# Attention head of a two-layer hybrid block: maxima of the first units spread over the projections of blocks one and two, later blocks projected beside the main line

## The chip, the cores and the metric

The kernel runs on one core of one Trainium2 chip. The metric is the device time of one launch in microseconds (us), as the median of several runs. The core has five engines with a queue each: TensorE (PE, with its weight loads shown apart as PEld), VectorE (DVE), ScalarE (ACT), GpSimd (POOL) and SyncE (SP), which here only issues DMAs. Matrix products land in PSUM, of which the kernel uses banks of 128 x 512 floats.

## The reference, cut to what matters

One sequence of 4096 rows of 256 features goes through attention, mixture of experts, attention, mixture of experts, each on a normalised input and added to its input. All is float32.

```python
def attn(x, Wq, Wk, Wv, Wo, bo, denom_bias):      # 16 heads of 16
    q, k, v = (split_heads(x @ W.T) for W in (Wq, Wk, Wv))
    sim = einsum('bhid,bhjd->bhij', q, k) / sqrt(16)
    sim = where(causal_mask, -max, sim)
    exp_sim = exp(sim - max(sim, -1))
    attn = exp_sim / (sum(exp_sim, -1) + exp(denom_bias))
    return merge_heads(attn @ v) @ Wo.T + bo
def ffn(x, phi_w, phi_b, expert_w, expert_b): ...  # soft mixture of 64 experts, 32 slots
x = x + attn_a(layernorm(x));  x = x + ffn(layernorm(x))
x = x + attn_b(layernorm(x));  x = x + ffn(layernorm(x))   # attn_b: no denom_bias, no bo
```

## The kernel before, in words

The four layers run one after the other on the same residual `x`, which stays in SBUF. The change touches only the class `_Attention`, which runs twice: attention a from about 0 to 1800 us and attention b from about 2650 to 4420 us of the profiled span.

**Blocks and units.** The 4096 rows are cut into eight blocks of 512. The 16 heads are cut into four groups of four. A unit is one group of heads of one block of query rows; the 32 units run block after block, four groups in each. A unit of block b looks at b + 1 key blocks, so the units grow.

**Projecting a block.** A block's rows are normalised, turned (8 transposes on PE), and multiplied by Wk, Wq and Wv: four `part`s, each two 128x512 products into one bank, and two `values`. Each `part` is split by ACT (L172) and DVE (L173) into a rounded and a rest term and written to DRAM (L175, L181), from where `load_to` (L337) reads it back in the layout of the scores, one 512 KB key tile or query tile at a time through SP's queue. `dense` (L234) is the list of seven steps that does this in one go, with the rows normalised on ACT. `pieces` (L186) is the same work as 16 small steps, with the rows normalised on POOL. These steps are put into `net.side`, and `net.beside` takes one of them at a time between the steps of the main line.

**Two passes over the scores.** `steps_a` (L359) computes the scores of a unit once for the row maxima: two 64-deep products into two banks, then two DVE reductions (L380 on the diagonal, L386 elsewhere) a step. After the last step `finish_a` turns the negated maxima and sends them through DRAM to the tile `qm`. `steps_b` (L438) computes the scores again into the tile `sc` with `-max` added by a second product, takes the exponential on ACT (L462), and `weigh` (L418) multiplies it with the values into `o`. So no unit's `steps_b` can begin before its maxima are done.

**Order around the change.** TensorE's instructions keep the order in which the program issues them (`net.mm` and `net.tr` pin it). The instructions of the other engines are placed by the framework's scheduler when their operands are ready. `wanted(n)` says how many steps of `steps_a` must be done by main step n; at n = 0 it is 16, the eight steps each of the first two units, which are both of block 0. Before the main line, `run` measures the rows (`net.stats` and `net.roots`, whose square root is on ACT), projects blocks 0 and 1 outright in attention a (`ready` is 0 there), and then runs blocks 2 and 3 as the list `front`, with one maxima step after each item. In attention b, blocks 0 and 1 were projected during the experts layer before (`ready` is 2), and `front` holds their values and blocks 2 and 3. In the main line, block b + 4 goes into `net.side` when block b begins. The banks of `steps_a`, of the projections and of the output product come from one pool of three; `sc` has two buffers.

Of the kernel before, what the change touches and what calls it, by code (L numbers as in the profile page):

```python
# [24 lines left out]
NQB = S // QB  # L25
# [17 lines left out]
class _Net:  # L43
# [5 lines left out]
    def __init__(self, ctx, tc, x, ident, eps):  # L49
        self.tc, self.nc = tc, tc.nc  # L50
        self.x, self.ident, self.eps = x, ident, eps
        pool = lambda n, b, **k: ctx.enter_context(tc.tile_pool(name=n, bufs=b, **k))
        cp = pool("net", 1)
        self.mv = cp.tile([P, NT, 2], F32, name="mv")
        self.rstd = cp.tile([P, NT], F32, name="rstd")
        self.shift = cp.tile([P, NT], F32, name="shift")

        self.zone = cp.tile([P, self.ZONE], F32, name="zone")
        self.stp = pool("stats", 4)
        self.ep = pool("ep", 1)  # L60
        self.dram = pool("dram", 1, space=DRAM)
        self.xds = [self.dram.tile([P, NT, D], F32, name=f"xd{n}") for n in range(2)]
        self.urgent, self.side = deque(), deque()
        self.agenda, self.now = [], 0
# [41 lines left out]
class _Attention:  # L106
# [12 lines left out]
    def __init__(self, net, name, wqT, wkT, wvT, woT, bo=None, db=None):  # L119
        self.net, self.name = net, name  # L120
        self.w = (wkT, wqT, wvT, woT)
        self.bo, self.db = bo, db
        self.kd, self.qd, self.ad = {}, {}, {}
        z = net.zone
        cut = lambda lo, n: z[:, lo : lo + n]
        self.wk, self.wq, self.wv = (
            cut(512 * n, 512).rearrange("p (c o) -> p c o", c=2) for n in range(3)
        )
        self.xb = [cut(1536 + 1024 * n, 1024).rearrange("p (c t) -> p c t", c=2) for n in range(2)]
        self.hl = [cut(3584 + 1024 * n, 1024).rearrange("p (l t) -> p l t", l=2) for n in range(2)]  # L130
        self.ys = [cut(5632 + 256 * n, 256) for n in range(2)]
        self.wo = cut(6144, 512).rearrange("p (c o) -> p c o", c=2)
        self.nhl = 0
        self.bot = None

    def load_weights(self):
# [49 lines left out]
    def pieces(self, b, fast=False, values=True):  # L186
        net, nc = self.net, self.net.nc
        xb, ys = self.xb[b % 2], {}
        idle = lambda: None

        def scale(i):
            if i == 0:
                self.begin(b)
            ys[i] = self.norm(4 * b + i, fast)

        def turn(t2):
            ps = net.bank().rearrange("p (c i t) -> p c i t", c=2, i=2)
            for i in range(2):
                for c in range(2):
                    net.tr(ps[:, c, i, :], ys[2 * t2 + i][:, ts(c, P)])  # L200
            nc.scalar.copy(xb[:, :, ts(t2, 2 * P)], ps.rearrange("p c i t -> p c (i t)"))

        def part(w, cc, key):
            ps = net.bank()
            for c in range(2):
                net.mm(ps, w[:, c, ts(cc, P)], xb[:, c, :], start=c == 0, stop=c == 1)
            self.split(ps, cc, (self.kd if key else self.qd)[b], key)

        out = []
        for t2 in range(2):  # L210
            out += [lambda i=i: scale(i) for i in (2 * t2, 2 * t2 + 1)]
            out += [idle, lambda t2=t2: turn(t2), idle]
        for w, key in ((self.wk, True), (self.wq, False)):
            out += [lambda a=(w, cc, key): part(*a) for cc in range(2)]
        if values:
            out += self.dense_values(b)
        return out
# [46 lines left out]
    def run(self, ready, at_end):  # L264

        net, tc, nc = self.net, self.net.tc, self.net.nc
# [3 lines left out]
        with ExitStack() as ctx:  # L270
# [13 lines left out]
                out=maskw, in_=maskw, compare_op=ALU.is_ge, fill=NEG,  # L284
# [11 lines left out]
            for p in range(2):  # L296
                f = net.ep.tile([P, QB], F32, name="ot", bufs=3)[:, 0:P]
                nc.gpsimd.memset(f, 0.0)
                for h2 in range(2):
                    for l in range(2):  # L300
                        nc.gpsimd.affine_select(
                            out=f, in_=f, compare_op=ALU.not_equal, fill=1.0,
# [34 lines left out]
            def load_to(n):  # L337
                while loaded[0] < min(n, len(kseq)):
                    u, kb = kseq[loaded[0]]
                    g, b = units[u]  # L340
                    if u not in qs:
                        q = qp.tile([P, 2, QB], F32R, name="q")
                        nc.sync.dma_start(
                            q.bitcast(F32),
                            self.qd[b][ts(g, HG)].bitcast(F32)
                            .rearrange("(p h) e l r t -> (h e l r) p t", p=2),
                        )
                        qs[u] = q
                    k = kp.tile([P, 2, QB], F32R, name="k")
                    nc.sync.dma_start(  # L350
                        k.bitcast(F32),
                        self.kd[kb][ts(g, HG)].bitcast(F32)
                        .rearrange("(p h) e r l t -> (h e r l) p t", p=2),
                    )
                    ks[u, kb] = k
                    loaded[0] += 1
# [77 lines left out]
            def values_to(n):  # L434
                while len(queue) > n:
                    weigh(queue.popleft())
# [107 lines left out]
            done_a = [0]  # L544

            def maxima_to(n):
                while done_a[0] < min(n, total):
                    next(runs)
                    done_a[0] += 1

            def wanted(n):
                for u in range(len(units)):
                    if due[u] > n:
                        lo, hi = due[u - 1], due[u]
                        first = ends[u - 1]
                        return first + -(-(ends[u] - first) * (n - lo) // (hi - lo))
                return total

            front = []
            if ready:  # L560
                for b in range(ready):
                    front += self.dense_values(b)
            else:
                for b in range(NQB):
                    for t in range(4 * b, 4 * b + 4):
                        net.stats(t)
                    net.roots(4 * b, 4 * b + 4)
                    if b < 2:
                        for f in self.dense(b, psb, prp):
                            f()  # L570
                    if b == 0:
                        load_to(1)
                if db is not None:
                    nc.scalar.activation(edb, edb, AF.Exp)
            for b in range(2, 4):
                front += self.dense(b, psb, prp)
            for f in front:
                f()
                maxima_to(min(done_a[0] + 1, wanted(0)))
            maxima_to(wanted(0))  # L580
            n = 0
            for u, (g, b) in enumerate(units):
                if g == 0 and 4 <= b + 4 < NQB:
                    net.side.extend(self.pieces(b + 4))
                if g == 0 and b == NQB - 1:
                    at_end()

                for p, _ in enumerate(steps_b(u)):
                    n += 1
                    if p % 2 == 0:  # L590
                        continue
                    while (
                        g >= 2 and net.side and u + 2 < len(units)
                        and units[u + 2][1] > max(3, b)
                    ):
                        net.beside()
                    want = wanted(n + 1)
                    maxima_to((done_a[0] + want) // 2)
                    values_to(1)
                    net.beside(2)  # L600
                    maxima_to(want)
# [555 lines left out]
```

## Time and profile before

| | |
|---|---|
| median of 3 runs | 5242.63 us (5239.64 to 5249.16) |
| the profiled execution | 5241.35 us, of which 5239.3 us from the first to the last instruction |
| PE busy | 5025.7 us (96% of the span) |
| DVE busy | 4141.6 us (79%) |
| ACT busy | 2633.1 us (50%) |
| mean granted TensorE clock | 0.982 |
| attention a: first main-line scores, last block ended | 84.5 us, 1793.5 us |
| attention b: first main-line scores, last block ended | 2717.4 us, 4412.3 us |

The profile has one row for an engine's group of instructions: the line of the kernel, the engine, the operation, the tile it writes and those it reads, how often, busy time, mean duration of one, and the idle time just before them with what ended it. A timeline row gives start, duration, engine, line, operation and tiles, and in brackets the idle time before it and its releaser. A row of a table by stage gives the stretch, its length, then the busy time (and number of instructions) of PE, PEld, DVE, ACT and, where all engines are asked for, POOL; then the granted TensorE clock as a share of full speed, the share of the DMA engines that were busy, and GB/s. A block's end is read from the copies of the finished output tile (L431), one a unit.

### The profile page before, as it was taken

What the parts mean: (1) busy time and instruction counts of PE and PEld (TensorE: products, weight loads), DVE (VectorE), ACT (ScalarE), POOL (GpSimd) and SP (SyncE); (2) the same over time, 40 slices, a digit from 0 to 9 for tenths busy, and PEclk for the clock granted to TensorE, in tenths of its full rate; (3) what the DMA queues carried; (4) which work ended last, traced back from release to release, by engine and by line L of the source; (5) the groups of instructions that cost most, each with busy time, mean ns of one, the idle gap of its engine ahead of it and who ended that gap; (6) DMA issues with size and microseconds to landing.
All of it is one profiled execution on the core that took longest, in us unless ns stands there. A gap on an engine that the chain in (4) does not pass through costs nothing.

```text
span 5239.3 us, 79442 instructions
## 1 busy us (share of the span) xinstructions
PE 5025.7 (96%) x29936; PEld 2683.4 (51%) x29936; DVE 4141.6 (79%) x7790; ACT 2633.1 (50%) x3108; POOL 1157.2 (22%) x1084
## 2 busy tenths in 40 slices
PE   7999999999999999989989999999999999999899
PEld 4444454445455344447754444545444553444488
DVE  5688989898989388767756889888889893787687
ACT  3466676766667622113224666766666676211132
POOL 3211100000000255534412111000000002555353
PEclk8999999999999999999999999999999999999999
DMA  6433222121121013433444332222121210134343
GB/s 252 140 107 127 67 73 68 61 67 61 59 64 53 32 78 104 148 127 114 144 175 144 107 127 67 72 68 64 64 64 57 64 53 31 77 105 147 122 148 111
DMA packets 266160, 499.16 MB, mean 95 GB/s; under 512 B 44944, under 2 KB 109968, under 8 KB 258096
## 3 DMA queue, kind: packets, MB, share of 16 engines
q1 hardware_dynamic: 260544, 485.57, 28.0%
q10 hardware_dynamic: 4896, 7.87, 0.4%
q8 instruction: 235, 3.85, 0.3%
q14 instruction: 149, 1.22, 0.1%
q0 software_dynamic: 336, 0.66, 0.1%
HBM read 336.73 MB, written 156.76 MB: 94 GB/s over the span
## 4 chain that ended last, share of the span: by engine, by line
PE 75%; DVE 11%; POOL 5%; issue 3%; ACT 3%; DMA 2%; SPq 0%; DVEq 0%; POOLq 0%; ACTq 0%
PE o L67 26%; PE bank L67 22%; PE sc L67 17%; PE acc L67 4%; DVE mx L386 4%; PE lg L67 4%; DVE junk L380 2%; POOL e L794 2%; PE ps L70 2%; POOL e L809 2%; ACT e L797 1%; DVE l L786 1%; ACT pb L462 1%; POOL e L826 1%; DMA zone<-ld 0%
## 5 line engine op out<-in xcount | busy, mean ns | idle before, releaser
L462 ACT ACTIVATE pb<-sc 128x1024 f32<-128x1024 f32 (+3 forms) x2304 | 2070.1, 950 | 1104.0 <-PE sc L67 1101.3
L386 DVE TENSOR_REDUCE mx<-bank 128x1 f32<-128x512 f32 x3584 | 2225.4, 682 | 179.5 <-PE bank L67 174.8
L67 PE MATMUL bank<-k,q 64*128 64x512 f32 (+3 forms) x4608 | 1354.7, 454 | 71.0 <-DVE mx L386 29.8
L67 PEld LDWEIGHTS bank<-k,q 64*128 64x128 f32 x4608 | 669.4, 186 | 1178.1 <-DVE mx L386 777.6
L67 PE MATMUL o<-pb,va 128*32 128x512 f32 (+3 forms) x9216 | 1160.4, 575 | 3.1 <-POOL pb L466 2.8
L67 PE MATMUL sc<-q,k 64*128 64x512 f32 (+3 forms) x4608 | 991.9, 391 | 9.6 <-ACT pb L462 9.2
L67 PE MATMUL sc<-qm,one 64*128 64x512 f32 (+3 forms) x4608 | 951.8, 378 | 0.0
L466 POOL TENSOR_SCALAR_AFFINE_SELECT pb<-pb 128x256 f32<-128x256 f32 x512 | 204.8, 407 | 2281.3 <-ACT pb L462 2275.5
L380 DVE CUSTOM_DVE_ANT_0 junk<-bank,maskw 128x128 bf16<-128x128 f32 (+3 forms) x1024 | 502.5, 491 | 258.9 <-PE bank L67 150.6
L67 PEld LDWEIGHTS sc<-q,k 64*128 64x128 f32 x4608 | 512.2, 187 | 138.2 <-ACT pb L462 98.9
L67 PEld LDWEIGHTS sc<-qm,one 64*128 64x128 f32 x4608 | 528.9, 187 | 67.7
L67 PE MATMUL acc<-e,x 128*128 128x512 f32 x1024 | 473.1, 605 | 19.3 <-POOL e L809 14.7
L797 ACT ACTIVATE e<-e 128x1024 f32<-128x1024 f32 x128 | 135.2, 1057 | 694.6 <-POOL e L794 694.6
L67 PE MATMUL lg<-zone,xnT 128*128 128x512 f32 x1024 | 463.3, 594 | 4.4 <-DVE l L786 3.8
L67 PE MATMUL o<-ys,lT 128*128 128x256 f32 x2048 | 464.9, 386 | 1.6 <-DVE xt L985 1.6
L67 PEld LDWEIGHTS o<-ys,lT 128*128 128x128 f32 x2048 | 392.6, 194 | 56.1 <-DVE xt L985 3.2
L826 POOL TENSOR_TENSOR e<-l,mc 128x1024 f32<-128x1024 f32 x120 | 281.3, 2365 | 319.5 <-DMA l<-ld 209.9
L67 PEld LDWEIGHTS o<-pb,va 128*32 128x32 f32 x9216 | 183.2, 108 | 290.6 <-issue 265.7
L67 PEld LDWEIGHTS acc<-e,x 128*128 128x128 f32 x1024 | 192.6, 193 | 265.5 <-issue 215.9
L809 POOL TENSOR_TENSOR e<-e,s 128x1024 f32<-128x1024 f32 x128 | 244.8, 1912 | 370.0 <-DVE s L808 348.5
L67 PEld LDWEIGHTS lg<-zone,xnT 128*128 128x128 f32 x1024 | 192.2, 190 | 245.7 <-issue 217.9
L807 DVE TENSOR_REDUCE s<-e 128x32 f32<-128x1024 f32 x128 | 156.1, 1219 | 155.2 <-ACT e L797 154.6
(122 smaller groups left out, 3208.4 us busy)
## 6 DMA issues: line engine op xcount, KB each, us to landing
k<-ak SPq DMA_DIRECT2D x144, 512.0 KB
k<-bk SPq DMA_DIRECT2D x144, 512.0 KB
ld<-l SPq DMA_DIRECT2D x128, 512.0 KB
l<-ld SPq DMA_DIRECT2D x60, 1024.0 KB
w<-in_L_ffn_expert_w_dram SPq DMA_DIRECT2D x26, 1024.0 KB
q<-aq SPq DMA_DIRECT2D x32, 512.0 KB
rb<-dd SPq DMA_DIRECT2D x64, 256.0 KB
q<-bq SPq DMA_DIRECT2D x32, 512.0 KB
```

The costliest lines, as they stand in the source:

```text
L67: self.tc.keep_in_program_order(self.nc.tensor.matmul(*a, **k))
L70: self.tc.keep_in_program_order(self.nc.tensor.transpose(o, i, self.ident))
L380: nc.vector.tensor_tensor_reduce(out=junk[:, 0:w], in0=scs[h2][:, 0:w], in1=maskw[:, QB - w : QB], scale=1.0, scalar=-3e38, op0=ALU.add, o ...
L386: nc.vector.tensor_reduce(m, scs[h2], AX.X, ALU.max)
L462: nc.scalar.activation(pb[:, :, off:QB], sc[:, :, off:QB], AF.Exp)
L466: nc.gpsimd.affine_select(out=d, in_=d, compare_op=ALU.is_ge, fill=0.0, base=0, pattern=[[0, 2], [1, P]], channel_multiplier=-1,)
L786: nc.vector.tensor_tensor(lf[:, ts(n, 512)], lg, phb[:, ds(h * EH + n * 512, 512)], ALU.add)
L794: nc.gpsimd.tensor_tensor(e, l, _bc(m.unsqueeze(2), [P, NH, SLOT]), ALU.subtract)
L797: nc.scalar.activation(ef, ef, AF.Exp)
L807: nc.vector.tensor_reduce(s, e, AX.X, ALU.add)
L809: nc.gpsimd.tensor_tensor(e, e, _bc(s.unsqueeze(2), [P, NH, SLOT]), ALU.mult)
L826: nc.gpsimd.tensor_tensor(e[:, ns, :], l, _bc(cms[t].unsqueeze(1), [P, NH, SLOT]), ALU.subtract)
```

## The change

The rows of blocks 3 to 7 of attention a are measured by a step of their own (`measure`) at the head of the block's `pieces`. Only block 0 is projected outright in attention a; blocks 1 and 2 form `front`, and the 16 maxima steps are spread evenly over its items. In attention b `front` is the values of blocks 0 and 1 and block 2. In the main line block b + 3 is projected beside block b, so block 3 moves from the head into block 0 of the main line, and each later block moves one block later. The amount of arithmetic stays the same.

```diff
@@ __init__
+        self.late = False
@@ pieces
-        out = []
+        def measure():
+            for t in range(4 * b, 4 * b + 4):
+                net.stats(t)
+            net.roots(4 * b, 4 * b + 4)
+
+        out = [measure] if self.late else []
@@ run
             else:
-                for b in range(NQB):
+                for b in range(3):
                     for t in range(4 * b, 4 * b + 4):
                         net.stats(t)
                     net.roots(4 * b, 4 * b + 4)
-                    if b < 2:
+                    if b == 0:
                         for f in self.dense(b, psb, prp):
                             f()
-                    if b == 0:
                         load_to(1)
+                self.late = True
                 if db is not None:
                     nc.scalar.activation(edb, edb, AF.Exp)
-            for b in range(2, 4):
+            for b in range(ready or 1, 3):
                 front += self.dense(b, psb, prp)
-            for f in front:
+            for n, f in enumerate(front):
                 f()
-                maxima_to(min(done_a[0] + 1, wanted(0)))
+                maxima_to(wanted(0) * (n + 1) // len(front))
             maxima_to(wanted(0))
             n = 0
             for u, (g, b) in enumerate(units):
-                if g == 0 and 4 <= b + 4 < NQB:
-                    net.side.extend(self.pieces(b + 4))
+                if g == 0 and b + 3 < NQB:
+                    net.side.extend(self.pieces(b + 3))
```

## The prediction

> **What bounds the kernel now.** I read the page first, then a table by stage (one row a block), then the timelines of PE and SP in the two heads.
>
> ```profile
> span 5239.3 us, 79442 instructions
> ...
> PE 5025.7 (96%) x29936; PEld 2683.4 (51%) x29936; DVE 4141.6 (79%) x7790; ACT 2633.1 (50%) x3108; POOL 1157.2 (22%) x1084
> ```
>
> PE is the bound: 214 us of the span are free of it, so a change that only moves PE work can win no more than the idle time it removes. Where is that idle time around the change?
>
> ```profile
> 28.50:42.70 14.20, 11.89 (x42) 6.90 (x40) 3.11 (x6) 7.10 (x13) 2.82 (x4) 1.00 1.03 385
> ...
> 85.00:100.00 15.00, 14.70 (x77) 8.00 (x73) 11.29 (x51) 5.20 (x8) 2.93 (x8) 0.56 0.21 76
> ...
> 84.50:165.40 80.90, 76.14 (x397) 38.84 (x397) 53.32 (x173) 28.71 (x45) 22.76 (x42) 0.73 0.39 132
> 443.90:642.00 198.10, 193.14 (x1356) 97.39 (x1353) 169.31 (x377) 125.17 (x148) 21.76 (x40) 1.00 0.33 105
> 642.00:870.60 228.60, 224.36 (x1636) 113.53 (x1633) 205.75 (x438) 151.34 (x173) 17.96 (x36) 1.00 0.22 69
> 1147.10:1465.10 318.00, 312.85 (x2276) 158.34 (x2273) 285.83 (x566) 213.45 (x237) 17.96 (x36) 0.99 0.20 63
> 2717.40:2791.60 74.20, 67.96 (x397) 35.64 (x396) 50.20 (x160) 30.74 (x48) 20.04 (x38) 0.84 0.43 135
> ```
>
> The first row is block 1 of attention a, projected outright: 14.2 us with 11.9 us of PE work. The next two show block 0 of a's main line at a granted clock of 0.56 and 0.73 while PE is hardly idle. The rows of blocks 3, 4 and 6 are the main line proper: PE idles about 5 us in each, with a projection beside it (block 3) or without (4 and 6). The last row is b's block 0: 6.7 us shorter than a's, at 0.84.
>
> ```profile
> 28.29 1.24 SPq L350 DMA_DIRECT2D k<-ak  x1
> 33.81 0.97 SPq L343 DMA_DIRECT2D q<-aq  x2
> ...
> 32.34 1.98 PE L67 MATMUL bank<-zone 128*128 128x512 f32 x4 [1.16 <-ACT zone L245]
> ...
> 44.96 0.33 PE L67 MATMUL bank<-k,q 64*128 64x128 f32 x2
> 46.18 1.98 PE L67 MATMUL bank<-zone 128*128 128x512 f32 x4 [0.89 <-ACT zone L245]
> ...
> 84.51 1.07 PE L67 MATMUL sc<-q,k 64*128 64x512 f32 x2
> ```
>
> This is a's head. The first query tile can only be asked for at 33.81, once block 0's queries are in DRAM. PE starts block 1's projections at 32.34, the first maxima at 44.96, the main line at 84.51.
>
> **Part 1, head of a.** The changed program's order on PE puts the first maxima right behind block 1's transposes, ahead of its first projection. PE keeps its order, so all of block 1's projections queue behind maxima that wait for the first key and query tile. When does the query land? Its issue takes half of 0.97 us, two 0.5 MB tiles are under way, and that stretch moves 385 GB/s, 1.3 us a tile: about 33.8 + 0.5 + 2.6 = 36.9, say 37. Bounds: 35.6 with one tile ahead, 40.3 if all five loads of that moment share the engines (6.5 us). The maxima of before began at 44.96 with no DMA named, so it cannot be later than that. From the first maxima on, before still did two blocks less one turn and 16 maxima steps; the changed head does the same. That took 84.51 - 44.96 = 39.55 us, of which 0.9 us was the wait for ACT's copy, done long before in the new order. So the main line starts near 37 + 38.65 = 75.7, a gain of 8.8 us (5.5 to 10.2) and not the 14.2 us of the block taken out: a wait of about 4.7 us (32.3 to 37) takes its place. Queued behind it on PE are block 1's projections, and with them ACT's and DVE's splits and SP's writes of that block; block 1's keys are first needed by the maxima of its own first unit, in the middle of block 0's main line, so only PE's own delay counts.
>
> **The clock after that wait.** What does such a gap do?
>
> ```profile
> 1810.49 6.05 PE L67 MATMUL acc<-e,x 128*128 128x512 f32 x8 [4.73 <-POOL e L809]
> ...
> 1808.40:1815.30 6.90, 4.81 (x6) 2.19 (x7) 5.37 (x7) 2.11 (x2) 4.98 (x4) 0.51 0.50 162
> ...
> 2361.24 1.02 PE L70 MATMUL ps<-ident,e 128*128 128x128 f32 x4 [2.03 <-DVE lT L884]
> ...
> 2361.40:2364.80 3.40, 3.40 (x11) 2.86 (x11) 3.40 (x6) 0.00 (x0) 0.56 (x1) 0.50 0.29 120
> ```
>
> A gap of 4.73 us is followed by some 5 us of work at half clock (0.51), one of 2.03 us by 3.4 us at 0.50. The Trainium skill, "TensorE: Matmul & The Clock Gate" (section "Why this matters for your kernels"), warns only of idle gaps over about 3 us, and holds some 4 us of continuous work enough for full clock. By the rule the new gap costs one slow stretch and no more. By the rows it costs 3.4 to 5 us at half rate, 1.7 to 2.5 us, and busy work is no protection: the row 85 to 100 is 98% busy and stays at 0.56. I take +1.7 us, and keep 0 and +7 (the difference of the two blocks 0 above) as ends for what shifted work does to the slow stretches.
>
> **Part 2, block 3 beside the main line.** Blocks 0 to 3 of the main line each had one projection beside them and still have one; block 4 gets one that it had not. PE works 96% and more of every block, so this costs about its PE time: 11.9 us by the row above. A second way: blocks 4 and 6, without side work, differ by 89.4 us or 44.7 a block, so block 3 without its side work would be 183.9; it took 198.1, hence 14.2. I take 12.5 us (11 to 14.5). Its DVE work (four splits of 0.69 us), ACT copies and POOL normalising (four of 1.23 and four of 0.73 us) lie in engines with 23 us and more of slack in that block. Its six DMA issues queue on SP, where block 3 carried the same six between its key loads. Sum for a: -8.8 + 1.7 + 12.5 = **+5.4 us**.
>
> **Part 3, `measure`.** Read from the source it would put a square root, and so two table loads (1.28 us each in the trace), between exponentials five times: 12.8 us of ACT. In the changed program's order all 32 row measurements on DVE and all eight roots on ACT still stand in the head, in the places of before, and ACT's count of table loads is unchanged. Cost zero, unless the chip's order were another; the cover is the scheduler.
>
> **Part 4, head of b.** Here keys and queries are loaded long before, so no wait appears.
>
> ```profile
> 2698.12 0.66 PE L70 MATMUL sc<-ident,zone 128*128 128x128 f32 x4
> ...
> 2717.37 0.50 PE L67 MATMUL sc<-q,k 64*128 64x512 f32 x2
> ...
> 2720.54 0.38 PE L67 MATMUL bank<-k,q 64*128 64x256 f32 x1 [0.25 <-DVE mx L380]
> 2721.11 0.38 PE L67 MATMUL bank<-k,q 64*128 64x256 f32 x1 [0.20 <-DVE mx L380]
> ```
>
> Block 3's stretch, 2698.12 to 2717.37, is 19.25 us and goes. Its maxima do not: 11 items now carry 16 steps, so five steps follow another maxima step directly, and there the three banks free up at DVE's pace, 0.57 us a bank at 256 wide (0.44 at 128 and 0.84 at 512 in the rows around it). A step is two banks; the five are 256, 512, 128, 384 and 512 wide: 1.15 + 1.6 + 0.9 + 1.35 + 1.6 = 6.6 us. Gain 19.25 - 6.6 = 12.6 us (11 to 14). Block 3 beside the main line costs 12.5 as in a. Sum for b: **-0.1 us**.
>
> **Total.** +5.3 us. Against the profiled execution (5239.3 span + 2.05 around it = 5241.35) that is 5246.7; the median of the runs shown is 1.3 us higher, so 5248.
>
> **Rivals.** (1) The slow clock spreads. After the wait PE runs at half rate into thin work, and b's first block, now behind paired maxima, starts cold as a's does (0.73 and not 0.84). Place: the first 80 us of each main line; price 6.7 us for b and up to 3 more for a's head, so about 5258, slower. For it: 98% busy work stayed at 0.56; b's slow stretch begins only at 0.51 around 2740. Against it: before's b also has waits of 0.7 us in every head step and keeps 1.00. It decides from one extra slow stretch of 13 us. (2) The slow clock shrinks: a's first block starts warm as b's does, gaining 6.7 us there and about as much in block 1 (122.3 us in a, 115.8 in b), and the new side work finds PE's idle time in block 4 (4.2 us). About 5235. For it: the lone maxima steps ahead of a's main line fall from two to one. Against it: the rest of that stretch is the same. (3) The change does nothing, because what leaves the head returns in full: then 5243 to 5245, the low half of my own case. (4) `measure` does land between the exponentials: +13 us or more; the order speaks against it.
>
> **How the numbers follow.** Chances: my sum 0.57, rival 1 0.25, rival 2 0.15, rival 4 0.03. My own case spans 5240 to 5256 from the bounds above. To leave out no more than 2 in 10 the range must take half of each rival: 5236 to 5262. A measurement of this kernel can tell about 0.2%, 10.5 us, from no change: below 5232 counts as faster, above 5253 as slower. From my case 0.17 lies above 5253 and 0.01 below 5232; rival 1 gives 0.21 above, rival 2 0.07 below, rival 4 lies above. Faster 0.08, same 0.51, slower 0.41.
>
> **What would show it.** In the profile after: PE's wait of 4 to 6 us before the first `bank<-k,q` row near 37 us; a's first `sc<-q,k` near 76 and b's about 26 us after its transposes of block 2 (39.4 before, from 2677.97); block 4 of both attentions longer by 11 to 14 us, near 241; blocks 3, 5 and 6 within 2 us; no new table load between exponentials. I am wrong if block 4 grows by under 8 us, if a's head gains over 12 us, or if the granted clock of the two blocks 0 moves by over 0.1.

## The result, and the profile after

The changed kernel takes 5253.05 us (median of 12 runs, 5246.8 to 5259.35) where the kernel before took 5238.93 us in the same measurement (12 runs, 5225.59 to 5249.16). The ratio is 1.0029, with a 95% interval of 1.002 to 1.0039: slower by 14 us (10.5 to 20.4), more than twice the forecast 5 us. The profiled execution took 5252.87 us; the kernel before had 5241.35.

The page of the changed kernel, engines' busy time (`...` marks lines left out, here and below):

```profile
span 5251.2 us, 79427 instructions
...
PE 5032.9 (96%) x29936; PEld 2684.6 (51%) x29936; DVE 4140.1 (79%) x7790; ACT 2629.6 (50%) x3102; POOL 1166.8 (22%) x1092
```

PE has the same 29936 instructions. Its busy time grew by 7.2 us and its idle time (span less busy) from 213.6 to 218.3 us. The change was to win idle time back; it added some. Where? The table by stage of the changed kernel (stretch, length, then busy time of PE, PEld, DVE, ACT and POOL, granted clock, DMA share, GB/s):

```profile
28.50:43.00 14.50, 6.08 (x19) 2.62 (x17) 0.93 (x6) 4.57 (x8) 2.81 (x4) 0.69 1.02 390
34.20:47.90 13.70, 8.65 (x14) 3.15 (x14) 1.71 (x9) 0.83 (x2) 0.00 (x0) 0.51 0.83 319
...
83.10:160.40 77.30, 70.77 (x388) 35.26 (x389) 52.79 (x172) 28.93 (x45) 23.25 (x43) 0.82 0.39 137
433.30:632.80 199.50, 194.60 (x1356) 98.18 (x1353) 169.45 (x377) 125.11 (x148) 25.59 (x44) 0.99 0.28 89
632.80:876.90 244.10, 238.60 (x1676) 120.99 (x1673) 208.55 (x442) 156.10 (x181) 21.76 (x40) 0.99 0.28 94
1150.60:1468.40 317.80, 312.72 (x2276) 158.52 (x2273) 285.68 (x566) 213.48 (x237) 17.94 (x36) 0.99 0.20 63
2710.90:2786.10 75.20, 68.86 (x397) 36.21 (x397) 52.62 (x170) 29.46 (x47) 20.04 (x38) 0.84 0.43 140
3258.80:3505.60 246.80, 239.09 (x1676) 120.83 (x1673) 208.05 (x438) 156.06 (x181) 20.35 (x38) 0.99 0.29 93
```

Rows one and two are a's head: PE does 6.08 us of work in 14.5 us, and then runs at a granted clock of 0.51 for 13.7 us. The rows that start at 433.30 and 1150.60 are blocks 3 and 6, as long as before (198.1 and 318.0). The rows at 632.80 and 3258.80 are block 4 of a and of b: 244.1 and 246.8 us where block 4 took 228.5 and 228.4. The rows at 83.10 and 2710.90 are the two blocks 0; b's kept its length and clock (74.2 us, 0.84).

The timeline of SP and that of PE in a's head, changed kernel:

```profile
33.68 0.99 SPq L350 DMA_DIRECT2D q<-aq  x2
34.72 0.46 SPq L357 DMA_DIRECT2D k<-ak  x1
```

```profile
38.85 0.47 PE L67 MATMUL bank<-k,q 64*128 64x128 f32 x2 [7.28 <-DMA q<-aq]
39.26 3.78 PE L67 MATMUL bank<-zone 128*128 128x512 f32 x4
...
43.84 3.78 PE L67 MATMUL bank<-zone 128*128 128x512 f32 x4 [0.39 <-DVE mx L387]
...
48.47 1.98 PE L67 MATMUL bank<-zone 128*128 128x512 f32 x4 [0.53 <-DVE mx L387]
...
57.33 1.99 PE L67 MATMUL bank<-zone 128*128 128x256 f32 x8 [0.65 <-DVE mx L387]
...
64.14 3.28 PE L67 MATMUL bank<-zone 128*128 128x512 f32 x4 [0.85 <-ACT zone L252]
...
83.10 0.73 PE L67 MATMUL sc<-q,k 64*128 64x512 f32 x2
```

The query tile asked for at 33.68 lets PE go on at 38.85, after a wait of 7.28 us. The same `part` (two products into a bank, `bank<-zone` 128x512 x4 here, as each product is two records) takes 3.78 us at half clock and 1.98 us at full clock: two parts right behind the wait are slow, and one more at 64.14 is slow in part (3.28 us). So the main line starts at 83.10, only 1.4 us earlier than before, although a block of 14.2 us has left the head.

The timeline of PE in b's head, changed kernel:

```profile
2685.92 0.66 PE L70 MATMUL sc<-ident,zone 128*128 128x128 f32 x4
...
2689.81 3.50 PE L67 MATMUL bank<-zone 128*128 128x512 f32 x4 [0.30 <-DVE mx L387]
...
2710.89 0.73 PE L67 MATMUL sc<-q,k 64*128 64x512 f32 x2
```

From the transposes of block 2 to the first scores it is 24.97 us, 39.4 before, although one part here too runs at half clock (3.50 us). What is block 4 paying? PE's groups in a's block 4 of the changed kernel (shapes, count, busy us and mean ns, idle time before and its releasers):

```profile
L67 PE MATMUL bank<-k,q 64*128 64x512 f32 x289 | 90.0, 473 | 5.1 <-DVE mx L393 3.5 <-DVE mx L387 0.3 <-DVE zone L175 0.2
...
L67 PE MATMUL bank<-zone 128*128 128x512 f32 x16 | 7.9, 618 | 0.0
...
L67 PE MATMUL bank<-zone 128*128 128x256 f32 x16 | 4.0, 392 | 0.0
...
L70 PE MATMUL bank<-ident,zone 128*128 128x128 f32 x8 | 1.3, 287 | 0.0
```

The last three rows are the new side work: 7.9 + 4.0 + 1.3 = 13.2 us of PE. PE's busy time in the block grew by 14.2 us (238.60 against 224.36); the maxima (the first row) ran 0.6 us longer and waited 1.4 us longer for their banks than in the kernel before:

```profile
L67 PE MATMUL bank<-k,q 64*128 64x512 f32 x289 | 89.4, 468 | 3.7 <-DVE mx L386 2.1 <-DVE mx L380 0.3
```

### The profile page after: what moved, and what is told of

Same layout as the page of the kernel before. It is cut to its first block, busy times and chain, and to the rows that moved or that the text cites. A ratio compares the mean times of both kernels' runs of the same rounds, so it can differ in the third digit from the quotient of the medians.

```text
span 5251.2 us, 79427 instructions
## 1 busy us (share of the span) xinstructions
PE 5032.9 (96%) x29936; PEld 2684.6 (51%) x29936; DVE 4140.1 (79%) x7790; ACT 2629.6 (50%) x3102; POOL 1166.8 (22%) x1092
## 4 chain that ended last, share of the span: by engine, by line
PE 75%; DVE 11%; POOL 4%; issue 3%; DMA 3%; ACT 3%; SPq 0%; DVEq 0%; POOLq 0%; ACTq 0%
PE o L67 26%; PE bank L67 22%; PE sc L67 17%; PE acc L67 5%; PE lg L67 4%; DVE mx L393 4%; DVE junk L387 2%; POOL e L802 2%; PE ps L70 2%; POOL e L817 1%; ACT e L805 1%; DVE l L794 1%; ACT pb L469 1%; DMA zone<-ld 1%; DMA l<-ld 1%
## 5 line engine op out<-in xcount | busy, mean ns | idle before, releaser
L67 PEld LDWEIGHTS lg<-zone,xnT 128*128 128x128 f32 x1024 | 192.3, 190 | 245.1 <-issue 219.0
```

The source lines that it names most:

```text
L67: self.tc.keep_in_program_order(self.nc.tensor.matmul(*a, **k))
```

## The experiments

Each kernel of the table was timed beside runs of the kernel before on the same chip; rows with the same median of before share those runs. One profile shows single stages to a few us only: two profiles of the unchanged kernel have a's block 0 at 80.9 and 76.4 us and a's end at 1793.5 and 1785.3. Block 4 (228.4 to 228.5 us in both attentions) and a's head (39.5 us from first maxima to first scores) repeat much better, and most verdicts rest on those. b's head took 47.7 us in one and 50.6 us in the other: in the second, two parts ran at half clock.

| kernel | median, us | before, us | ratio (95%) | first scores of a | a's block 4 | b's head | b's block 4 |
|---|---|---|---|---|---|---|---|
| before | 5238.93 | | | 84.5 | 228.5 | 47.7 | 228.4 |
| changed | 5253.05 | 5238.93 | 1.0029 (1.002 to 1.0039) | 83.1 | 244.0 | 34.1 | 246.8 |
| e1, b alone | 5240.04 | 5237.1 | 1.0004 (0.9996 to 1.0013) | 85.8 | 229.5 | 34.0 | 243.6 |
| e2, a alone | 5250.23 | 5237.1 | 1.0029 (1.0015 to 1.0043) | 84.3 | 246.3 | 47.7 | 228.6 |
| e3, no wait | 5248.16 | 5237.1 | 1.0022 (1.0015 to 1.003) | 73.1 | 243.9 | 33.9 | 245.4 |
| e5, warm gap | 5256.58 | 5237.1 | 1.0036 (1.0024 to 1.0049) | 83.9 | 245.1 | 34.2 | 246.4 |
| e4, side work twice | 5268.26 | 5235.03 | 1.0061 (1.0048 to 1.0073) | 85.3 | 243.5 | 47.7 | 244.6 |
| e6, spread alone | 5246.57 | 5235.03 | 1.0024 (1.0017 to 1.003) | 88.3 | 228.4 | 45.5 | 228.2 |
| e7, warm gap, old pacing | 5246.85 | 5235.03 | 1.0025 (1.0017 to 1.0033) | 77.8 | 248.4 | 32.5 | 247.8 |
| e8, all in the head | 5258.72 | 5235.03 | 1.0043 (1.003 to 1.0055) | 140.9 | 229.8 | 106.0 | 228.6 |
| e9, before again | 5237.79 | 5236.76 | 0.9999 (0.9991 to 1.0007) | 85.5 | 228.5 | 50.6 | 228.4 |
| e10, spread in a | 5240.94 | 5236.76 | 1.0005 (0.9997 to 1.0013) | 91.0 | 228.6 | 47.7 | 228.2 |
| e11, change, old pacing in a | 5250.41 | 5236.76 | 1.0029 (1.0019 to 1.004) | 79.9 | 243.6 | 34.2 | 245.1 |

The columns of block 4 and of b's head are in us; b's head runs from its first maxima to its first scores.

**One attention at a time.** e1 keeps attention a as before and changes b; e2 does the reverse. Of e1 (e2 swaps the conditions, and has the changed head in a):

```diff
-            for b in range(2, 4):
+            for b in range(2, 3 if ready else 4):
...
-                maxima_to(min(done_a[0] + 1, wanted(0)))
+                maxima_to(
+                    wanted(0) * (n + 1) // len(front) if ready
+                    else min(done_a[0] + 1, wanted(0))
+                )
...
-                if g == 0 and 4 <= b + 4 < NQB:
-                    net.side.extend(self.pieces(b + 4))
+                ahead = 3 if ready else 4
+                if g == 0 and b + ahead < NQB:
+                    net.side.extend(self.pieces(b + ahead))
```

> Attention b as in the changed kernel, attention a as before. Theory (each attention trades a cheaper head for 15 to 18 us of projections beside block 4): b alone is +7 us, near 1.0013, with its first scores about 34 us after its first maxima (47.7 before) and its block 4 at 245 us. Rival (the loss is a's late query and slow clock alone): b alone is within 2 us of before.

> Attention a as in the changed kernel, attention b as before. Theory: +6 us, near 1.0011; a's first scores near 83, its block 4 at 244 us, and this and the other half add up to the +14 us of the whole. Rival (the loss is b's): within 2 us of before.

Measured: b alone costs 2 us (-2 to 7), a alone 15 us (8 to 23), and together they make up the whole. Neither 7 nor 6 us came: b's half is what its rival said, and nearly all of the loss is a's. In e2's profile the main line starts at 84.34 and block 4 is 246.3 us: the block came back and the head gave nothing for it. In b the head gives 13.7 us and block 4 takes 15 to 18 us, a little more than that.

**The wait taken out.** e3 is the changed kernel with a's maxima begun only when block 1's projections have been issued, seven items later, so that the query has landed by then:

```diff
-                maxima_to(wanted(0) * (n + 1) // len(front))
+                skip = 0 if ready else 7
+                maxima_to(wanted(0) * max(0, n + 1 - skip) // (len(front) - skip))
```

> The changed kernel, but in attention a no maxima step is issued until block 1 is projected; all 16 are spread over block 2's seven items. So nothing of block 1 queues behind the first query tile. Theory (the wait of 7.3 us and the half clock after it ate the head's gain): a's first scores near 75 in place of 83.1, and the total 8 us under the changed kernel, near 5245. Rival (PE idle time only moves: nine more paired maxima steps wait for banks at 1.3 us each, and thin work turns the clock down anyway): first scores at 80 to 84, total within 3 us of the changed kernel.

Measured: 5248.16, by the ratios some 4 us under the changed kernel, where 8 were expected, and still 11 us (8 to 16) over before. The profiled execution took 5240.49 us, one of e3's quickest, so only its stages are read here. PE's timeline and its stage row in e3:

```profile
46.10 0.43 PE L67 MATMUL bank<-k,q 64*128 64x128 f32 x3
...
73.07 1.08 PE L67 MATMUL sc<-q,k 64*128 64x512 f32 x2
```

```profile
46.10:73.10 27.00, 20.65 (x66) 9.95 (x65) 16.49 (x66) 5.81 (x8) 4.42 (x5) 1.00 1.03 380
```

Without the wait the clock stays at 1.00 and the main line starts at 73.07, 12 us ahead of before. So the wait and the half clock in the head cost the changed kernel 10 us there. But block 4 still takes its 15 us more, and that is over what even this head gives.

**The gap kept warm.** e5 is the changed kernel with eight useless products (7 us of PE) in the place of the idle wait:

```diff
+                if n == 0 and not ready:
+                    warm = psb.tile([P, 2, QB], F32, name="sc")
+                    for _ in range(8):
+                        mm(
+                            warm[:, 0, :], self.wk[:, 0, 0:P], self.xb[0][:, 0, :],
+                            start=True, stop=True,
+                        )
```

> The changed kernel with eight products of no use (128x512, 6.9 us at full clock, result dropped) put on PE into a's wait for the first query tile. Theory (the wait turned the clock down): the first two projections after it take 1.98 us each and not 3.78, the granted clock from 30 to 48 us stays at 1.00, a's first scores come at 78 to 79 in place of 83.1; total 4 us under the changed kernel. Rival (the thin interleaved work itself turns the clock down): half clock there as before, first scores at 83 or later.

The timeline of PE and a stage row of e5:

```profile
32.27 7.03 PE L67 MATMUL sc<-zone 128*128 128x512 f32 x16
39.23 0.33 PE L67 MATMUL bank<-k,q 64*128 64x128 f32 x2
39.49 1.99 PE L67 MATMUL bank<-zone 128*128 128x512 f32 x4
...
53.79 1.99 PE L67 MATMUL bank<-zone 128*128 128x256 f32 x8 [0.66 <-DVE mx L387]
55.72 0.50 PE L67 MATMUL bank<-k,q 64*128 64x512 f32 x2
56.46 1.04 PE L67 MATMUL bank<-k,q 64*128 64x512 f32 x2 [0.24 <-ACT va L235]
...
60.60 3.78 PE L67 MATMUL bank<-zone 128*128 128x512 f32 x4 [0.85 <-ACT zone L252]
```

```profile
60.00:74.00 14.00, 12.49 (x18) 4.29 (x18) 3.27 (x17) 1.92 (x4) 3.84 (x5) 0.51 0.69 269
```

The first part behind the gap is now fast (1.99 us), so it was the idle wait that had slowed it. Yet the half clock comes 20 us later, at 60, where PE had no gap over 0.85 us, and the main line starts no earlier (83.86). Nor is the total the 4 us lower that were expected. Something else in the new head turns the clock down. What differs from the head of before at that place is the pacing: the even spread puts two maxima steps in a row (55.72 and 56.46) ahead of block 2's transposes, so between the end of the last projection (53.79 + 1.99 = 55.78) and the next (60.60) lie 4.8 us of maxima and transposes alone. In the kernel before it was 62.47 to 66.00, 3.5 us:

```profile
60.48 1.99 PE L67 MATMUL bank<-zone 128*128 128x256 f32 x8 [0.66 <-DVE mx L380]
...
66.00 1.98 PE L67 MATMUL bank<-zone 128*128 128x512 f32 x4 [0.68 <-ACT zone L245]
```

**The spread alone, and the old pacing.** Four kernels test that. e6 is the kernel before with the spread alone; e10 has it in a only; e7 is e5 with the old pacing in a; e11 is the changed kernel with the old pacing in a and nothing warmed. e6's edit, and that of e11 (e10 and e7 are made of the same lines):

```diff
-                maxima_to(min(done_a[0] + 1, wanted(0)))
+                maxima_to(wanted(0) * (n + 1) // len(front))
```

```diff
-                maxima_to(wanted(0) * (n + 1) // len(front))
+                maxima_to(
+                    wanted(0) * (n + 1) // len(front) if ready
+                    else min(done_a[0] + 1, wanted(0))
+                )
```

> The kernel before, with only the maxima spread evenly over the projections of blocks two and three (one step after each second or so item to the end, instead of one after each item until all are done); the same blocks are projected in the heads. Theory: the spread by itself brings nothing, -1 to 0 us, first scores of a 0 to 1 us earlier. Rival (the clock decides): thinner interleaving at the end turns PE's clock down in other places, and block 0 of a's main line moves by over 3 us either way.

> The kernel before with the even spread of the maxima in attention a alone; b keeps one step after each item. Theory (the spread costs through the half clock it brings to a's head, 68 to 75 us in the profile with the spread in both): first scores of a 42 to 43 us after the first maxima instead of 39.5, total 3 to 11 us over before, as much as with the spread in both. Rival (b's spread is what costs): total within 2 us of before.

> The changed kernel with the useless products in a's wait and, in a, the old pacing of the maxima (one step after each item, so no two steps stand directly before block 2's turn). Theory (the paired maxima with the turn turn the clock down near 60 us): no stretch at half clock at 60 to 74 us, first scores near 78 us, total 5 us under the changed kernel, about 5248. Rival (it is the thin work of maxima between projections as such): the half clock comes at another place of the head, first scores at 82 us or later, total 5253 to 5257.

> The changed kernel with the old pacing of the maxima in a (one step after each item until done), nothing warmed. Theory (the spread cost a some 8 us, and the prediction had put it at nothing): about 8 us under the changed kernel, 5243 to 5246 where before has 5236; the half clock after the wait stays (34 to 48 us), the one at 65 us goes, first scores near 79 to 80 us. Rival (the wait turns the clock down anyhow, and the pacing is of no account): first scores at 83 us, total within 3 us of the changed kernel, ratio to before 1.0025 or more.

The timeline of PE in e6, then in e11, then a stage row of e7:

```profile
60.96 2.00 PE L67 MATMUL bank<-zone 128*128 128x256 f32 x8 [0.66 <-DVE mx L380]
...
67.78 2.96 PE L67 MATMUL bank<-zone 128*128 128x512 f32 x4 [0.85 <-ACT zone L245]
...
71.53 3.78 PE L67 MATMUL bank<-zone 128*128 128x512 f32 x4 [0.39 <-DVE mx L380]
```

```profile
39.20 0.47 PE L67 MATMUL bank<-k,q 64*128 64x128 f32 x2 [7.88 <-DMA q<-aq]
39.60 3.78 PE L67 MATMUL bank<-zone 128*128 128x512 f32 x4
...
55.86 1.99 PE L67 MATMUL bank<-zone 128*128 128x256 f32 x8 [0.65 <-DVE mx L387]
...
61.38 1.98 PE L67 MATMUL bank<-zone 128*128 128x512 f32 x4 [0.68 <-ACT zone L252]
...
79.88 0.73 PE L67 MATMUL sc<-q,k 64*128 64x512 f32 x2
```

```profile
60.00:74.00 14.00, 11.53 (x38) 5.32 (x37) 7.66 (x30) 2.93 (x5) 2.55 (x3) 1.00 0.88 343
```

In e6, the kernel before with nothing but the new pacing, the pause is 62.96 to 67.78 (4.8 us) and two parts behind it are slow (2.96 and 3.78 us instead of 1.98). In e11 and e7, the pause is 3.5 us (57.85 to 61.38 in e11) and the clock stays up. At this place, the second turn to a new block in a's head, every profile agrees: with the spread begun at a's first item (changed, e2, e5, e6, e10) the half clock comes, at 60 to 71 us, five times out of five; with the old pacing (before, e1, e4, e7, e8, e9, e11) never.

The length of the pause alone does not decide, though. In e3 a pause of 4.1 us (57.27 to 61.38) left the clock at 1.00. And e10 fell to half clock already at 47, behind the pause of 3.25 us (43.01 to 46.25) one block earlier, where before, e1, e4, e6, e8 and e9, whose program is the same up to there, did not. The timeline of PE in e10:

```profile
46.25 2.93 PE L67 MATMUL bank<-zone 128*128 128x512 f32 x4 [0.89 <-ACT zone L245]
...
49.98 3.78 PE L67 MATMUL bank<-zone 128*128 128x512 f32 x4 [0.39 <-DVE mx L380]
```

Of the 45 pauses of 3.2 to 3.7 us in the heads of the thirteen profiles, four were followed by half clock (e10 here, e8 in both heads, e9 in b's). In b's head with the change the pause is 4.2 us, and half clock follows in five profiles of six; in the sixth, e7, the head is some 1.5 us shorter. Over these profiles, then, a longer pause makes half clock likelier, and chance has a part.

In a, the pacing moves the first scores by some 2 to 6 us: 77.80 against 83.86 (e7 and e5), 88.3 against 85.5 (e6 and e9). Of the 3.2 us between e11 and the changed kernel (79.88 and 83.10), 1.8 belong to half clock that lasted longer behind the wait, and of the 5.5 us of e10 (91.0) some 2.8 to the two slow parts above.

The Trainium skill, "TensorE: Matmul & The Clock Gate" (section "Part 1: The HAM clock gate (the "warmup" mystery)"), says that the gate watches PE's activity in free-running windows of some 3.4 us. The record of the granted clock agrees: half-clock stretches here last 3.4 us or a multiple of it (6.8, 10.2, 13.7 us). A pause of 4.8 us can fill such a window with light work, and one of 3.2 to 3.5 us only where it happens to lie right; that this is the reason is my reading, only the effect of the pacing at that place is shown.

The totals don't resolve 4 us. By their ratios e7 is 13 us over before where e5 was 19, but only 2 us under the changed kernel, where 5 were expected. e11 missed: 5243 to 5246 was expected, 5250.4 measured, no different from the changed kernel within the intervals (10 to 21 us over before, against 10.5 to 20.4), although its trace does what the theory said. e6's theory, -1 to 0 us, fell, and its total is a riddle: 12.6 us over before (9 to 16), of which its stages show 3 to 4 in a's head and none in b (its b head is even 2.2 us shorter), while e10, with the same spread in a, measures 3 us (-2 to 7), which cannot choose between its theory (3 to 11) and its rival (within 2). That remainder is open.

**The price of a side block.** e4 is the kernel before with block 7 projected a second time beside block 4. In attention a its second projection takes rows to which the output bias has been added, and adds it once more, so this kernel's output is not the reference's; the work on the engines is that of one more block.

```diff
                 if g == 0 and 4 <= b + 4 < NQB:
                     net.side.extend(self.pieces(b + 4))
+                if g == 0 and b == 4:
+                    net.side.extend(self.pieces(7))
```

> The kernel before, with block 7 projected a second time beside block 4 of both attentions (the same values are written again): nothing is taken out of the heads, so this is the price of one more block of projections beside the main line by itself. Theory (side work costs its PE time plus its waits for banks): block 4 longer by 15.4 to 18 us in each attention, 31 to 34 us in all, ratio 1.006. The prediction's figure (12.5 us each): 25 us, ratio 1.0048. If block 4's idle time of 4 us took part of it: under 22 us.

The rows by stage of the two blocks 4 in e4:

```profile
636.40:879.90 243.50, 237.94 (x1676) 120.23 (x1673) 208.26 (x441) 155.98 (x180) 21.79 (x40) 1.00 0.29 95
3272.30:3516.90 244.60, 238.63 (x1674) 121.20 (x1673) 207.98 (x438) 156.21 (x181) 20.45 (x38) 0.99 0.28 94
```

With both heads untouched, block 4 grows by 15.0 and 16.2 us, and the total by 32 us (25 to 38). So a side block costs some 16 us by itself, not the 12.5 of the prediction. Over all profiles with it (seven for each attention), block 4 is 16.1 us longer in a and 17.3 in b than in those without.

**The other way round.** If a block costs 16 us beside block 4 and 14 in the head, should all of them be in the head? e8 is the kernel before with no side work at all:

```diff
-            for b in range(2, 4):
+            for b in range(2, NQB):
...
-                if g == 0 and 4 <= b + 4 < NQB:
-                    net.side.extend(self.pieces(b + 4))
```

> The kernel before, turned the other way: all blocks from the third on are projected in the heads between the maxima, and none beside the main line. Theory (a block costs 15.4 to 18 us beside the main line and some 14.2 us in the head): four blocks in two attentions, each block of the main line from 0 to 3 shorter by some 16 us, heads longer by 57 us each, 5 us or more saved per attention: 5227 to 5231, ratio 0.998. Rival (in the head the projections are bound by their loads and run at a lower clock, and blocks 0 to 3 have less PE work to hide their own waits): same or slower, 5240 to 5260.

Rows by stage of e8, b's head first and then blocks 3 and 4 of a, and blocks 3 and 4 of a in the second profile of before (e9):

```profile
2670.50:2776.50 106.00, 88.48 (x297) 48.52 (x296) 32.68 (x96) 39.97 (x67) 0.00 (x0) 0.97 0.79 299
455.00:643.90 188.90, 182.73 (x1316) 91.51 (x1313) 166.62 (x374) 120.38 (x141) 17.95 (x36) 0.99 0.22 72
643.90:873.70 229.80, 225.22 (x1636) 114.55 (x1633) 205.69 (x438) 151.36 (x173) 17.93 (x36) 0.99 0.21 68
```

```profile
437.50:635.70 198.20, 193.23 (x1355) 97.64 (x1352) 169.39 (x378) 125.33 (x149) 21.78 (x40) 1.00 0.32 105
635.70:864.20 228.50, 224.22 (x1634) 113.54 (x1632) 205.60 (x437) 151.32 (x173) 17.96 (x36) 1.00 0.21 69
```

The theory fell: e8 is 22.5 us slower (16 to 29). The heads grow by 56 us in a (95.7 against 39.6 us from first maxima to first scores) and 55 to 58 in b, some 14 us a block, as expected. But block 3 without its side work is only 9.3 us shorter, since its own products ran longer: PE's busy time fell by 10.5 us where 13.2 us of side work left. Over a, blocks 0 to 3 together give back 49 us against the mean of the profiles with the old head and pacing, and over b 36 (12 and 9 us a block), where 64 each was expected. A block's projections thus cost about 9 us beside block 3, 14 in the head and 16 to 17 beside block 4. The kernel before has its blocks at the cheapest of the three places; why the price differs between blocks 3 and 4 was not settled.

**The same program twice.**

> The kernel before once more, unchanged: it gives a second profile of it, taken on the chip of these runs, and shows how far two measurements of one program differ. Theory: ratio 1.000 within 0.001; first scores of attention a 39.5 us after the first maxima, blocks 3 and 4 at 198 and 228.5 us; the time between the attentions within 5 us of 876. Rival (the differences of 0.2 % seen so far lie within what the same program shows): ratio off 1 by 0.002 or more.

Measured: 0.9999 (0.9991 to 1.0007), as expected, so this repeat gives no sign that the intervals are too narrow. The head and blocks 3 and 4 of a repeat; the time from a's end to b's first maxima was 879.7 against 876.2 us.

## Why the prediction was right or wrong

The direction of the sum was right and its size was not: 14 us and not 5, so that a difference put as too small to tell is one that can be told (0.29%). The measured time lies inside the range given (5236 to 5262) because that range was wide; it lies on the mark (5253) above which the prediction counts the kernel as slower. The terms, by the profiles of before and after:

- **a's head, forecast -8.8 + 1.7 us; measured -1.4 (-2.4 against the second profile of before).** This step failed, in three places. The query let PE go at 38.85 and not at 37: 4.7 us after the end of its issue instead of 2.6, about midway to the upper bound, in which all five loads share the engines (40.3, or 40.8 with the half us of issue that the bound leaves out); which loads delayed it was not measured. The wait is 7.28 us, not 4.7. The clock behind it cost two slow parts of 1.8 us each, and not the 1.7 us that the nearest rows, of shorter gaps, suggested. And the step "the changed head does the same" overlooked, in its 38.65 us, the pacing: the spread brings a second slow stretch near 65. From first maxima to first scores it took 44.25 us: 5.6 more than reckoned, of which the three slow parts are 1.8 + 1.8 + 1.3 = 4.9. With 1.85 us for the later landing that is the whole 7.4 us.
- **Block 3 beside a's main line, forecast +12.5; measured +15.5, and 16.1 over all profiles.** The term was mis-sized: its 11.9 us came from the projection in the head, where the products run back to back; as side work the same 32 records of products and 8 transposes read 13.2 us in their groups. The rest is what I had put at nothing in the body of the estimate: maxima that find their bank taken, and a little longer products. e4 shows the price alone. The second way, by the difference of blocks 4 and 6, gave 14.2 and was nearer.
- **b's head, forecast -12.6; measured -13.6.** Right as a sum, with some luck: half clock at block 2, in no term of mine, cost about 1.5 us (3.50 instead of 1.99 for one part), and e7, which escaped it, gains 15.2. So the paired maxima cost less than the 6.6 us reckoned, about 4.
- **Block 3 beside b's main line, forecast +12.5; measured +18.4, and 17.3 over all profiles.** Mis-sized as in a.
- **`measure`, forecast 0; right.** The square roots all stayed in the head, with ACT's count of table loads unchanged, so rival 4 fell.

The measured terms add to -1.4 + 15.5 - 13.6 + 18.4 = +18.9 us, a little over the measured 14 and inside its interval (10.5 to 20.4); the other stages move by the few us that two profiles of one program show.

Rival 1, the slow clock spreading, was right on its mechanism and wrong on its place: it costs a's head some 5 us, and leaves the two blocks 0 alone (b's keeps 0.84; a's went from 0.73 to 0.82, which the second profile of before has too). Rival 2 fell: no block 0 is warmer than before's own profiles show, and the side work found no idle time, as PE idles 5.5 us in a's block 4 where it idled 4.2. Rival 3, that all that leaves the head returns, is nearest to what attention a did, but more returns than left. Even with the wait and the half clock of a's head gone (e3) that head gives 12 us and block 4 takes 15, and e3 is still 11 us slower than before: the clock in a's head is not all of the loss.

## What to carry to other kernels

Price moved work at both ends by rows of the same kind: what a stage gives back when work leaves it, and what it costs to add it at the new place, can differ by several us for the same projections (9, 14 and 16 us here), and a PE that is busy for 98% of a stage, as here in block 4, has no room to hide it. When PE work is queued behind a load, price the landing with all the transfers of that moment, and expect the slow clock to outlast the wait (here by 5 to 9 us). Where thin work sits between bursts of products, keep the pauses between the bursts short: an innocent change of pacing turned the clock down here.

## What the runs showed of the hardware

- Behind a wait of 7.28 us (31.6 to 38.85) PE ran at half clock: it began in the wait, at 34, and ended at 47.6 us, 8.8 us after the wait (0.51 over 34.2 to 47.9). With the same wait in e2 (7.69 us) and e11 (7.88 us) it ended 4.8 us after it. PE was busy for most of that time.
- Half clock also came without any gap over 0.85 us, behind 4.8 us of maxima and transposes (e5, 0.51 for 13.7 us; five profiles of five). Behind 3.2 to 3.7 us of them it came 4 times in 45, and the same program had it in one execution and not in another (b's head in e9 and in before).
- Eight useless products in a wait did keep the clock up behind it (1.99 us a part instead of 3.78, in e5 and e7); under the even spread of e5 the time so won was lost again 20 us later.
